# Context values from seven block products instead of eight, and the next batch's key products begun one pass early

## Chip, core and metric

The kernel runs on one core of a Trainium2 chip. The metric is device time in microseconds (us) of one execution, measured from run to run on the chip; smaller is better. A core has TensorE (PE: matmuls into PSUM, with weight loads shown apart as PEld), VectorE (DVE), ScalarE (ACT), GpSimd (POOL) and SyncE (SP), each with an instruction stream of its own that runs in order; they wait for one another through semaphores. Transfers between HBM and SBUF are issued here from SP (plain ones) and from POOL (those that add to what lies in SBUF).

## What is computed

One layer of a perceiver in f32: cross-attention from 16 x 64 query rows to 16 x 1024 context rows, self-attention, and a feed-forward part with quantized weights. The change lies in the keys and values of the cross-attention. Cut to that:

```python
def _L0_xattn_ref(query, key, value, Wq, Wk, Wv, Wo):   # key = value = ctx_4096
    b, sq, _ = query.shape                               # 16, 64, 1024
    _, sk, _ = key.shape                                 # 1024
    q = (query @ Wq).reshape(b, sq, 32, 32).transpose(0, 2, 1, 3)
    k = (key @ Wk).reshape(b, sk, 8, 32).transpose(0, 2, 1, 3)
    v = (value @ Wv).reshape(b, sk, 8, 32).transpose(0, 2, 1, 3)
    k, v = jnp.repeat(k, 4, axis=1), jnp.repeat(v, 4, axis=1)
    probs = jax.nn.softmax(jnp.einsum('bhqd,bhkd->bhqk', q, k) * 32 ** -0.5, axis=-1)
    out = jnp.einsum('bhqk,bhkd->bhqd', probs, v).transpose(0, 2, 1, 3).reshape(b, sq, 1024)
    return out @ Wo
x = x + _L0_xattn_ref(_layernorm(x), ctx_4096, ctx_4096, Wq, Wk, Wv, Wo)
```

Wk and Wv are 1024 x 256. For each of the 16 batches, `ctx @ Wk` and `ctx @ Wv` are products of 1024 x 1024 by 1024 x 256.

## The kernel before

**Passes.** The attention loop (`for n in range(2 * B)`, line 1100) runs 32 passes, two for each batch b = n // 2: an even one for the first half of the heads (g = 0) and an odd one for the second. A pass has four parts, i = 0 to 3. In a pass the kernel finishes the softmax of unit n and makes the scores of unit n + 1 (`following.by_key(i)`, matmuls of line 575). Of the scores, ScalarE copies one half (L587) while VectorE takes maxima (L591, L594), and then they change halves. After i = 3, `reduce` and `spread` send the maxima through HBM (`tops`) and bring them back to all partitions. In parts 1 and 2 of the next pass VectorE subtracts them (L618), ScalarE takes exponentials (L619), and GpSimd adds them up (`sums`: L625, L628). `values` (L637) multiplies probabilities with the context values: waves 0 and 1 in part 2, waves 2 and 3 in part 0 of the next pass, followed by `finish` (L647) and `quotients` (L656 to L666).

**Fillers.** Between these parts the kernel puts the projection of the next batch's keys and values in small steps: `fill(n)` takes n steps from a list. A step is about 1.7 us of matmuls. A pass takes 15 of them (`fill(2)` at line 1163 and `fill(1 if i == 0 and fast else 2)` at line 1178).

**Keys and values of a batch** (`project_fast`, line 388; 14 of the 16 batches). The context lies in HBM as `ctxT[b, h]`, h the half of its rows, with 8 blocks of 128 input features; `quarter(b, h, i)` is four blocks of one half, 1 MB. The keys are a 2 x 2 block product and are made by seven block products (`z5, p1, p2, z6, z7, p3, z4`, line 407) in place of eight, from sums of weight blocks (`w_sums`) and two sums of context quarters: `chained`, which grows from one quarter to four, and `paired`, of two. These sums are made by transfers that add in SBUF (`add_to_chain`, `add_to_pair`, issued from GpSimd, L381 and L384). p1 and p2 share a PSUM bank, as do z5 and p3; the rest is put together by VectorE (L445, L453, L458, L463) and GpSimd (L446). The values are made plainly (line 426): for each of 8 row tiles, 8 matmuls of 256 columns, copied by ScalarE (L434). They read the whole halves, `load_context` (L232, 2 MB each). A product is two steps, a row tile of values two.

**Order by hand.** Everything is in a manual schedule: the order in which the code emits instructions is the order on each engine. In even passes `held_back` moves `sums(1)` and `sums(2)` behind `add_to_chain(b + 1, 0, 1)` at line 1182.

**Places.** SBUF is one arena and `place(kb, shape)` a region at a fixed KB: `chained` 8, `paired` 16, `w_sums` 24, four key and value buffers from 32, the two 16 KB context halves (`stream`) at 64 and 80, the weights `wkvs` at 96. PSUM banks 0 and 1 are tags m0 and m1 and bank 2 is t1; t0 holds the outputs, w0 and w1 the scores.

**The end.** In passes 30 and 31 the fillers are `project_out` (the output projection; four steps for each of tile t and half h), 32 steps for 32 places.

Of the kernel before, what the change touches and what calls it, by code (L numbers as in the profile page):

```python
# [15 lines left out]
ALU = mybir.AluOpType  # L16
# [4 lines left out]
P = 128  # L21
DIM = 1024
B = 16
# [3 lines left out]
KC = DIM // P  # L27
HD = 32
KVD = 256
# [20 lines left out]
def kernel(  # L50
# [156 lines left out]
    chained, paired = (place(kb, [4, 512]) for kb in (8, 16))  # L207
    w_sums = place(24, [4, 4, P])
# [153 lines left out]
    def weight_sums():  # L362
        b11, b21 = (wkvs[:, 4 * i : 4 * i + 4, 0:P] for i in range(2))
        b12, b22 = (wkvs[:, 4 * i : 4 * i + 4, P : 2 * P] for i in range(2))
        s, t, z7, z4 = (w_sums[:, i] for i in range(4))
        nc.vector.tensor_tensor(s, b11, b12, ALU.subtract)
        nc.vector.tensor_tensor(z7, b12, b22, ALU.subtract)
        nc.vector.tensor_tensor(t, b22, s, ALU.add)
        nc.vector.tensor_tensor(z4, b21, t, ALU.subtract)

    def quarter(b, h, i):
        return ctxT[b, h, :, 4 * i : 4 * i + 4, :]

    def begin_chain(b):
        nc.sync.dma_start(chained, quarter(b, 1, 0))

    def begin_pair(b):
        nc.sync.dma_start(paired, quarter(b, 1, 0))

    def add_to_chain(b, h, i):  # L380
        nc.gpsimd.dma_start(chained, quarter(b, h, i), accum_op=ALU.add)  # L381

    def add_to_pair(b):
        nc.gpsimd.dma_start(paired, quarter(b, 0, 0), accum_op=ALU.add)  # L384

    later = []

    def project_fast(b):

        kT = kv_ring.next([2, NK])  # L390
        v = kv_ring.next([8, KVD])
        x_bank, z_bank, y_bank = (i % 3 for i in range(b % 3, b % 3 + 3))
        held = {}
        k11, k12, k21, k22 = (
            kT[:, g, bass.ts(h, 512)] for h, g in ((0, 0), (0, 1), (1, 0), (1, 1))
        )
        b11, b21 = (wkvs[:, 4 * i : 4 * i + 4, 0:P] for i in range(2))
        b22 = wkvs[:, 4:8, P : 2 * P]
        s, t, w7, w4 = (w_sums[:, i] for i in range(4))
        whole = lambda h, i: ctx_halves[b, h][:, 4 * i : 4 * i + 4, :]  # L400

        def product(name, n, weights, what, done, first=True):
            def piece(i):
                if i == 0 and first:
                    held[n] = bank(n, f"{name}_{b}")
                for k in (2 * i, 2 * i + 1):
                    nc.tensor.matmul(  # L407
                        held[n],
                        lhsT=weights[:, k, :],
                        rhs=what()[:, k, :],  # L410
                        start=(first and k == 0),
                        stop=(k == 3),
                        skip_group_check=not first,
                    )
                if i == 1:
                    done(held[n])

            return [lambda: piece(0), lambda: piece(1)]

        def values(h, kts, n):  # L420
            def piece(i):
                if i == 0:
                    held[n] = bank(n, f"v_{b}_{h}_{kts[0]}")
                at, half = divmod(i, 2)
                for k in range(4 * half, 4 * half + 4):
                    nc.tensor.matmul(  # L426
                        held[n][:, bass.ts(at, KVD)],
                        lhsT=ctx_halves[b, h][:, k, bass.ts(kts[at], P)],
                        rhs=wkvs[:, k, KVD:],
                        start=(k == 0),  # L430
                        stop=(k == KC - 1),
                    )
                if i == 2 * len(kts) - 1:
                    nc.scalar.copy(  # L434
                        v[:, h * 4 + kts[0] : h * 4 + kts[-1] + 1, :],
                        held[n].rearrange("p (k c) -> p k c", c=KVD)[:, : len(kts)],
                    )

            return [lambda i=i: piece(i) for i in range(2 * len(kts))]

        def copy(out):
            return lambda ps: nc.scalar.copy(out, ps)  # L442

        def after_z7(ps):
            nc.vector.tensor_tensor(k21, ps, k12, ALU.subtract)  # L445
            nc.gpsimd.tensor_tensor(k22, k21, k22, ALU.subtract)  # L446

        z5 = product("z5", z_bank, s, lambda: chained, copy(k22))
        p1 = product("p1", x_bank, b11, lambda: whole(0, 0), copy(k12))
        p2 = product("p2", x_bank, b21, lambda: whole(0, 1), copy(k11), first=False)  # L450
        z6 = product(
            "z6", y_bank, t, lambda: chained,
            lambda ps: later.append(lambda: nc.vector.tensor_tensor(k12, k12, ps, ALU.subtract)),  # L453
        )
        z7 = product("z7", y_bank, w7, lambda: paired, after_z7)
        p3 = product(
            "p3", z_bank, b22, lambda: chained,
            lambda ps: nc.vector.tensor_tensor(k12, ps, k12, ALU.add),  # L458
            first=False,
        )  # L460
        z4 = product(
            "z4", x_bank, w4, lambda: whole(1, 1),
            lambda ps: nc.vector.tensor_tensor(k21, ps, k21, ALU.add),  # L463
        )
        steps = z5 + p1 + values(0, (0,), y_bank) + p2 + z6 + values(0, (1, 2), x_bank)
        steps += z7 + p3 + z4 + values(0, (3,), y_bank)
        steps += values(1, (0, 1), z_bank) + values(1, (2, 3), x_bank)
        return kT, v, steps

# [592 lines left out]
    with tc.manual_schedule():  # L1062
# [37 lines left out]
        for n in range(2 * B):  # L1100

            b = n // 2
            if n % 2 == 0:
                fill(len(fillers))
                if b == 0:
                    load_context(1, 1)
                    kT, v, key_steps, value_steps = project(1)
                    for h in range(2):

                        for step in key_steps[h] + value_steps[h]:  # L1110
                            fillers += [step, lambda: None]
                elif b + 1 < B:
                    kT, v, steps = project_fast(b + 1)
                    fillers += steps
                if b + 1 < B:
                    tiles.append((kT, v))
                else:
                    for t in range(4):
                        load_x(xs[t], t)
                    for h in range(2):  # L1120
                        for t in (4, 5):
                            fillers += project_out(t, h)
                    for t in (0, 1):
                        for h in range(2):
                            fillers += project_out(t, h)
            following = Unit(n + 1, *tiles[(n + 1) // 2]) if n + 1 < 2 * B else None

            for i in range(4):
# [8 lines left out]
                if i == 2 and n == 2 * B - 3:  # L1137
                    wos.append(load(wo[0]))
# [4 lines left out]
                if not odd and fast:  # L1143
                    if i == 2:
                        load_context(b + 1, 1)
                if odd and b + 2 < B:
                    if i == 1:
                        begin_chain(b + 2)
                    if i == 2:
                        load_context(b + 2, 0)  # L1150
                        begin_pair(b + 2)
                if n == 1 and i == 1:
                    weight_sums()
# [6 lines left out]
                if n == 2 * B - 3 and i == 2:  # L1160
                    for t in (4, 5, 0, 1, 2, 3):
                        nc.sync.dma_start(outputs[t].rearrange("p g r c -> p (g r c)"), results[t])
                fill(2)
                if i == 0 and not odd and fast:
                    add_to_chain(b + 1, 0, 0)
# [3 lines left out]
                if i in (1, 2) and following:  # L1169
                    unit.exponentials(2 * i - 2)  # L1170
                    if i == 1 or not held_back:
                        unit.sums(2 * i - 2)
                if i == 1 and not odd and fast:
                    add_to_pair(b + 1)
# [3 lines left out]
                fill(1 if i == 0 and fast else 2)  # L1178
                if n < 8 and i == 0:
                    treat_piece()  # L1180
                if i == 2 and held_back:
                    add_to_chain(b + 1, 0, 1)
                    unit.sums(1)
                    unit.sums(2)
                if i == 1 and odd and b + 2 < B:
                    add_to_chain(b + 2, 1, 1)
# [6 lines left out]
                if i in (1, 2) and following:  # L1193
                    unit.exponentials(2 * i - 1)
                    if i == 2 or not held_back:
                        unit.sums(2 * i - 1)
                while later:
                    later.pop(0)()
# [226 lines left out]
```

## Time and profile before

Three runs took 1863.46, 1866.37 and 1866.81 us, the median 1866.37. The profiled execution has a span of 1863.3 us, from its first to its last instruction.

| what | us or share |
|---|---|
| median of the runs | 1866.37 |
| span of the profiled execution | 1863.3 |
| first scores made in pass 0 | at 186.1 |
| one batch (two passes), 9 of them in a row from 524 on | 70.2 |
| passes 2 to 9, where these two passes took longer | 72.7 to 79.8 |
| start of pass 30, the first of the last batch | 1226.8 |
| context transfers of 1 MB from POOL | 56, 11.4 from issue to landing |

How to read it: "busy" is the share of the span in which an engine had an instruction running. Matmuls are pipelined, and the end of each is modelled, so a matmul's mean is longer than the spacing between two of them. Each f32 matmul leaves two records in the trace and two weight loads. A timeline line gives start, length, engine, line, operation and count, and merges neighbours of one line. A line such as "L426 PE MATMUL v<-arena 128*128 128x256 f32 x1792 | 405.2, 382" is a group: rows times columns of the array, output form, count, busy us and mean ns of one, and after the next bar the engine's idle time ahead of the group and what ended it.

### The profile page before, as it was taken

To read this page: it belongs to the slowest core of one execution; us is meant where nothing else is said; L and a number is where in the kernel's file an instruction comes from. 1 tells how busy PE (TensorE), PEld (TensorE's weight loads), DVE (VectorE), ACT (ScalarE), POOL (GpSimd) and SP (SyncE) were. 2 spreads that over 40 slices of the span, in tenths; PEclk is the share of its full clock that TensorE was granted. 3 is DMA by queue.
4 is the path that set the end of the run, shared out by engine and by line. 5 is a ranking of instruction groups with operands and counts; after the bars stand their busy time and mean duration, and the time that the engine had idled before them with its cause. 6 is when DMAs were issued, how large, how long until landed. Compare 5 with 4: busy or idle time off the path is not lost.

```text
span 1863.3 us, 26374 instructions
## 1 busy us (share of the span) xinstructions
PE 1822.5 (98%) x10880; PEld 1080.9 (58%) x10880; DVE 1219.1 (65%) x1436; ACT 926.5 (50%) x988; POOL 885.8 (48%) x505
## 2 busy tenths in 40 slices
PE   8999999999899999999999999999999999899999
PEld 5445565565565665665665665664446454566654
DVE  3011587777877887887887887877524257775554
ACT  1233656665566776776776776544101123664221
POOL 1000446655565576576566566565503424455520
PEclk9999999999999999999999999999999999899999
DMA  9234578777687787886787787663120032243201
GB/s 346 69 106 139 187 223 271 224 231 237 188 262 196 253 254 191 263 254 195 254 252 201 251 254 202 198 186 153 36 75 19 1 77 62 51 130 109 75 29 51
DMA packets 64264, 314.65 MB, mean 169 GB/s; under 512 B 10192, under 2 KB 19344, under 8 KB 47376
## 3 DMA queue, kind: packets, MB, share of 16 engines
q1 hardware_dynamic: 52848, 242.99, 37.1%
q0 software_dynamic: 10144, 67.88, 17.2%
q10 hardware_dynamic: 1152, 2.10, 0.3%
q8 instruction: 85, 1.39, 0.3%
q14 instruction: 35, 0.29, 0.0%
HBM read 293.74 MB, written 19.20 MB: 168 GB/s over the span
## 4 chain that ended last, share of the span: by engine, by line
PE 66%; DVE 2%; POOL 2%; ACT 1%; DMA 1%; issue 1%; ACTq 0%; POOLq 0%; DVEq 0%
PE v L426 15%; PE z L407 10%; PE wo L250 6%; PE t L575 5%; PE q L250 5%; PE o L637 5%; PE d L1040 4%; PE p L407 4%; PE g L961 3%; PE gu L961 3%; PE v L740 1%; PE k L250 1%; POOL arena L628 1%; DMA arena<-in_ctxT 1%; PE o L647 1%
## 5 line engine op out<-in xcount | busy, mean ns | idle before, releaser
L628 POOL TENSOR_TENSOR arena<-arena 128x1024 f32<-128x1024 f32 x192 | 541.7, 2821 | 20.5 <-ACT arena L619 8.5
L426 PE MATMUL v<-arena 128*128 128x256 f32 x1792 | 405.2, 382 | 1.2 <-ACT arena L442 1.2
L594 DVE TENSOR_TENSOR arena<-t,arena 128x512 f32<-128x512 f32 x384 | 258.9, 688 | 211.6 <-PE t L575 155.3
L426 PEld LDWEIGHTS v<-arena 128*128 128x128 f32 x1792 | 336.8, 190 | 78.6 <-issue 29.5
L618 DVE TENSOR_TENSOR arena<-arena 128x2048 f32<-128x2048 f32 x128 | 373.5, 2958 | 4.3 <-DMA arena<-tops 4.3
L587 ACT COPY arena<-t 128x1024 f32<-128x1024 f32 x256 | 254.8, 1009 | 209.1 <-PE t L575 118.0
L619 ACT ACTIVATE arena<-arena 128x2048 f32<-128x2048 f32 x128 | 244.6, 1911 | 168.6 <-DVE arena L618 167.8
L625 POOL TENSOR_TENSOR arena<-arena 128x1024 f32<-128x1024 f32 x32 | 75.8, 2368 | 524.6 <-ACT arena L619 491.1
L407 PE MATMUL z<-arena 128*128 128x512 f32 x560 | 260.6, 608 | 11.3 <-ACT arena L442 5.3
L250 PE MATMUL q<-arena 128*128 128x512 f32 x512 | 224.6, 595 | 0.6 <-ACT arena L287 0.6
L407 PEld LDWEIGHTS z<-arena 128*128 128x128 f32 x560 | 103.2, 192 | 138.1 <-issue 117.5
L250 PEld LDWEIGHTS q<-arena 128*128 128x128 f32 x512 | 95.6, 190 | 116.4 <-issue 114.3
L575 PE MATMUL t<-arena 32*128 32x256 f32 x2048 | 146.6, 400 | 1.3 <-ACT arena L346 1.2
L961 PEld LDWEIGHTS <-arena 128*128 128x128 bf16 x1024 | 98.8, 98 | 64.7 <-issue 13.7
L591 DVE TENSOR_REDUCE arena<-t 128x512 f32<-128x1024 f32 x64 | 74.7, 1204 | 90.9 <-PE t L575 90.9
L575 PEld LDWEIGHTS t<-arena 32*128 32x128 f32 x2048 | 93.1, 184 | 66.6 <-issue 61.4
L637 PE MATMUL o<-arena 128*32 128x256 f32 x2048 | 123.8, 382 | 0.0
L250 PE MATMUL wo<-arena 128*128 128x512 f32 x256 | 112.3, 595 | 0.3 <-ACT arena L287 0.3
L407 PE MATMUL p<-arena 128*128 128x512 f32 x224 | 108.2, 605 | 0.0
L637 PEld LDWEIGHTS o<-arena 128*32 128x32 f32 x2048 | 60.0, 109 | 68.7 <-issue 32.0
L722 POOL TENSOR_TENSOR arena<-arena 128x512 f32<-128x512 f32 x20 | 33.5, 1673 | 133.6 <-DVE arena L720 133.6
L961 PE MATMUL gu<-arena 128*128 128x344 fp8e4 x544 | 85.3, 314 | 9.6 <-ACT arena L969 6.5
(146 smaller groups left out, 1974.6 us busy)
## 6 DMA issues: line engine op xcount, KB each, us to landing
arena<-in_ctxT SPq DMA_DIRECT2D x31, 2048.0 KB, 11.4
arena<-in_ctxT POOLq DMA_DIRECT2D x56, 1024.0 KB, 11.4
arena<-in_ctxT SPq DMA_DIRECT2D x28, 1024.0 KB, 12.1
arena<-tops SPq DMA_DIRECT2D x48, 512.0 KB, 4.9
arena<-in_wg SPq DMA_DIRECT2D x32, 688.0 KB, 4.5
arena<-in_wu SPq DMA_DIRECT2D x32, 688.0 KB, 6.2
arena<-in_wd SPq DMA_DIRECT2D x32, 688.0 KB, 9.2
arena<-ternary POOLq DMA_DIRECT2D x26, 344.0 KB, 3.8
```

The costliest lines, as they stand in the source:

```text
L250: nc.tensor.matmul(made[0], lhsT=lhsT(k), rhs=rhs(k), start=(k == 0), stop=(k == KC - 1))
L407: nc.tensor.matmul(held[n], lhsT=weights[:, k, :], rhs=what()[:, k, :], start=(first and k == 0), stop=(k == 3), skip_group_check=not first,)
L426: nc.tensor.matmul(held[n][:, bass.ts(at, KVD)], lhsT=ctx_halves[b, h][:, k, bass.ts(kts[at], P)], rhs=wkvs[:, k, KVD:], start=(k == 0), s ...
L575: nc.tensor.matmul(ws[jj // 2][:, jj % 2, a, :], lhsT=self.kT[rows, self.g, bass.ts(i * 2 + a, P)], rhs=two_tiles[self.b // 2 % 2][rows, s ...
L587: nc.scalar.copy(pt[:, 2 * mine : 2 * mine + 2], ws[mine])
L594: nc.vector.tensor_tensor(m, w[:, :, a], m, ALU.max)
L618: nc.vector.tensor_tensor(pt, pt, by.to_broadcast([P, 4, 2, 256]), ALU.subtract)
L619: nc.scalar.activation(pt, pt, AF.Exp)
L625: nc.gpsimd.tensor_tensor(acc, pt[:, :, 0], pt[:, :, 1], ALU.add)
L628: nc.gpsimd.tensor_tensor(acc, acc, pt[:, :, a], ALU.add)
L637: nc.tensor.matmul(self.po[bass.ts(jj, HD), 0:256], lhsT=self.v[:, kt, bass.ts(self.g * 4 + jj, HD)], rhs=self.pts[i][:, jj, a, :], start= ...
L961: nc.tensor.matmul(ps[:, :CW], lhsT=xqT[t][:, k, :], rhs=wbs[n][i][:, k, :], start=(k == 0), stop=(k == KC - 1),)
```

## The change

The values are made like the keys. `products(kind, then)` builds the seven products for keys (kind 0) and for values (kind 1). For values the context is the stationary operand as before, but each product covers one quarter of the input features and 128 output columns: for each of 4 row tiles, 4 matmuls with 128 columns. There is a second set of weight sums (`w_sums[1]`), and the block b11 of both kinds is negated in place once.

Four products of each kind, p1, z6, z7 and z4, are added up in one PSUM bank one after the other; ScalarE reads the bank after each. z5 is kept apart (`fifths`). p2 and p3 are added to the results by VectorE, and after z6 and z7 GpSimd adds or subtracts z5.

No whole half is loaded any more. Each batch loads four quarters from SP (`load_quarter`) and adds four from GpSimd (`add_quarter`), each issued when the product that last read the place is done (`then`). There are two `chains`, for even and odd batches.

The first two key products of batch b + 2 (z5, p1) become the last four steps of the passes of batch b. A pass has 14 steps in place of 15; the second `fill` of part 0 takes none. In even passes `sums(0)` comes after the second fill of part 1, and the other sums directly follow their exponentials. With the last fast batch, `project_out(4, 0)` takes the place of the products begun early; its inputs are loaded earlier.

```diff
-    chained, paired = (place(kb, [4, 512]) for kb in (8, 16))
-    w_sums = place(24, [4, 4, P])
+    chains = [place(kb, [4, 512]) for kb in (64, 8)]
+    paired, second_in, last_in = (place(kb, [4, 512]) for kb in (16, 72, 80))
+    w_sums = [place(kb, [4, 4, P]) for kb in (24, 88)]
+    fifths = [place(kb, [512]) for kb in (172, 174)]
...
+    def negate_first(kind):
+        b11 = weight_block(kind, 0, 0)
+        nc.scalar.mul(b11, b11, -1.0)
...
+    def load_quarter(dst, b, h, i):
+        if b < B:
+            nc.sync.dma_start(dst, quarter(b, h, i))
+    def add_quarter(dst, b, h, i):
+        if b < B:
+            nc.gpsimd.dma_start(dst, quarter(b, h, i), accum_op=ALU.add)
...
+                else:
+                    for kt in (2 * i, 2 * i + 1):
+                        for k in range(4):
+                            nc.tensor.matmul(
+                                ps[:, bass.ts(kt, P)],
+                                lhsT=what[:, k, bass.ts(kt, P)],
+                                rhs=weights[:, k, :],
+                                start=(first and kt == 0 and k == 0),
+                                stop=(k == 3),
+                                skip_group_check=True,
+                            )
...
+            sums = kind
+            free = (2, sums)[kind]
+            def copied(out, scale=1.0):
+                return lambda ps: nc.scalar.mul(out, ps, scale)
+            def added(out):
+                return lambda ps: nc.vector.tensor_tensor(out, ps, out, ALU.add)
+            def after_z6(ps):
+                nc.scalar.mul(o12, ps, -1.0)
+                nc.gpsimd.tensor_tensor(o12, o12, fifth, ALU.add)
+            def after_z7(ps):
+                nc.scalar.copy(o22, ps)
+                nc.gpsimd.tensor_tensor(o22, o22, fifth, ALU.subtract)
...
+                "z5": made("z5", free, s, chain, copied(fifth)),
+                "p1": made("p1", sums, b11, paired, copied(o11, -1.0)),
+                "p2": made("p2", 2, b21, second_in, added(o11)),
+                "z6": made("z6", sums, t, chain, after_z6, False),
+                "z7": made("z7", sums, w7, paired, after_z7, False),
+                "z4": made("z4", sums, w4, last_in, copied(o21), False),
+                "p3": made("p3", (2, 0)[kind], b22, chain, added(o12)),
...
+                "z6": lambda: load_quarter(second_in, b + 1, 0, 1),
+                "z4": lambda: load_quarter(paired, b + 1, 0, 0),
+                "p3": lambda: load_quarter(last_in, b + 1, 1, 1),
...
+                "z5": lambda: add_quarter(chain, b, 0, 0),
+                "p1": lambda: add_quarter(paired, b, 1, 0),
+                "p2": lambda: load_quarter(chain_of(b + 1), b + 1, 1, 0),
+                "z6": lambda: add_quarter(chain, b, 0, 1),
+                "z7": lambda: add_quarter(chain_of(b + 1), b + 1, 1, 1),
...
+        order = [values["z5"], keys["p2"], values["p1"], values["p2"], keys["z6"], values["z6"]]
+        order += [keys["z7"], values["z7"], keys["z4"], values["z4"], keys["p3"], values["p3"]]
+        return kT, v, keys["z5"] + keys["p1"], sum(order, [])
...
-                    kT, v, steps = project_fast(b + 1)
-                    fillers += steps
+                    kT, v, early_steps, steps = begun or project_fast(b + 1)
+                    fillers += steps if begun else early_steps + steps
+                    begun = project_fast(b + 2) if b + 2 < B else None
+                    if begun:
+                        fillers += begun[2]
+                    else:
+                        fillers += project_out(4, 0)
...
+                if n == 2 and i == 0:
+                    negate_first(0)
+                    weight_sums(1)
+                    negate_first(1)
+                    load_quarter(last_in, 2, 1, 1)
...
                 if i in (1, 2) and following:
                     unit.exponentials(2 * i - 2)
-                    if i == 1 or not held_back:
+                    if i == 2 or not held_back:
                         unit.sums(2 * i - 2)
...
-                fill(1 if i == 0 and fast else 2)
+                fill(0 if i == 0 and fast and b > 1 else 2)
+                if i == 1 and held_back:
+                    unit.sums(0)
...
-                if i == 2 and held_back:
-                    add_to_chain(b + 1, 0, 1)
-                    unit.sums(1)
-                    unit.sums(2)
...
                     unit.exponentials(2 * i - 1)
-                    if i == 2 or not held_back:
-                        unit.sums(2 * i - 1)
+                    unit.sums(2 * i - 1)
```

## The prediction

> **What bounds the kernel now.** I read the page's busy shares first, then the stretches, the chain of waits and the timelines of one batch. A batch is two of the 32 passes; T is the moment when TensorE starts the first scores (by_key, i = 0) of an even pass, 910.42 in the batch quoted.
>
> ```profile
> PE 1822.5 (98%) x10880; PEld 1080.9 (58%) x10880; DVE 1219.1 (65%) x1436; ACT 926.5 (50%) x988; POOL 885.8 (48%) x505
> ...
> 446.80:524.00 77.20, 71.28 (x438) 43.97 (x437) 57.75 (x63) 41.84 (x42) 43.72 (x23) 0.96 0.68 195
> ...
> 877.50:947.70 70.20, 70.20 (x458) 44.39 (x457) 57.69 (x59) 48.74 (x43) 44.36 (x22) 1.00 0.78 236
> ```
>
> The columns after the stretch are its length and the busy time of TensorE, its weight loads, VectorE, ScalarE and GpSimd, then granted clock, DMA share and GB/s. A steady batch lasts 70.20 us and TensorE is busy for all of it; VectorE has 12.5 us left, ScalarE and GpSimd over 20. Only early batches differ: 446.8 to 524.0 has 5.9 us without TensorE work and a clock of 0.96. So TensorE sets the time, and the chain of waits runs along it:
>
> ```profile
> 922.23 3.45 PE v L426 x16
> ...
> 930.38 3.43 PE z L407 x8
> ```
>
> Each matmul leaves two records. A 512-column record costs 3.43/8 = 0.429 us, a 256-column one 3.45/16 = 0.216. A batch holds 56 key records and 128 value records: 24.0 + 27.6 us.
>
> **Part 1, the value matmuls.** Eight products of 8 matmuls with 256 columns become seven products of 16 matmuls with 128 columns: 128 records go, 224 come. The trace has no f32 multiply with 128 columns; the nearest is a transpose of the same shape, with as many weight loads:
>
> ```profile
> 38.78 1.04 PE L285 MATMUL n1p<-ident,arena 128*128 128x128 f32 x8
> ...
> L426 PEld LDWEIGHTS v<-arena 128*128 128x128 f32 x1792 | 336.8, 190 | 78.6 <-issue 29.5 <-ACT arena L442 3.7 <-DVE arena L594 3.4
> ```
>
> Eight in 1.04 us, less the last one's modelled 0.27, leave 7 spacings of 0.110 us. The lower bound is half of 0.216, 0.108. The upper bound is a load of a value matmul shown as 190 ns, if it cannot hide: 0.190. Two loads following each other at 963.463 and 963.571 are 0.108 apart though the first is shown as long as 0.186, so the shown length is not the spacing. I take 0.110: 224 x 0.110 = 24.6 against 27.6, **3.0 us a batch less**, 14 batches, **-42 us**. At 0.190 it would be 42.6, +15.0 a batch, +210 us.
>
> [...]
>
> **Part 2, work off TensorE.** VectorE had four 0.68 us key sums a batch (L445, L453, L458, L463) and has four additions of the same shape (p2, p3 for keys and values): 0. ScalarE had three key copies (0.59) and five value copies (three of 0.58, two of 0.35), 4.2 us; it gets ten of 0.59, 5.9: +1.7. GpSimd had one L446 of 1.28 and gets four: +3.8; its four DMA issues stay four. On SP, two 2 MB and two 1 MB loads become four 1 MB loads. Against idle times of 12 to 26 us a batch these sizes are covered by TensorE; at nothing, unless an order makes them late. On SP each quarter is now issued behind the product that frees its place, ahead of later transfers of the maxima (tops), which wait for later scores anyway. The tightest is the first-half quarter for p1: issued when key z4 ends, 11.6 us into the odd pass, landed by the median 12.0 at 23.6, needed at 29.7. Uncovered, its 6.1 us of slack would have to go first; 0.
>
> **Part 3, the order on GpSimd.** Before, sums(1) to sums(3) of an even pass were put behind the accumulating transfers. Now they go ahead of the one that p3 needs. Queue of an even pass: transfer for z6, transfer for z7, sums(0), sums(1), sums(2), key z6 addition, sums(3), value z6 addition, **transfer for p3**, key z7, value z7, transfer for the next z5. Behind the late one wait the z7 additions and the next z5's transfer; those have 5 us to spare.
>
> ```profile
> L628 POOL TENSOR_TENSOR arena<-arena 128x1024 f32<-128x1024 f32 x192 | 541.7, 2821 | 20.5 <-ACT arena L619 8.5
> ...
> L618 DVE TENSOR_TENSOR arena<-arena 128x2048 f32<-128x2048 f32 x128 | 373.5, 2958 | 4.3 <-DMA arena<-tops 4.3
> ...
> 968.89 7.30 DVE L618 TENSOR_TENSOR arena<-arena 128x2048 f32<-128x2048 f32 x2
> ...
> 967.01 18.73 POOL L628 TENSOR_TENSOR arena<-arena 128x1024 f32<-128x1024 f32 x6
> ...
> DMA to landing us min/median/max: 9.1/11.9/16.7
> ```
>
> Where L618 and L628 meet, each loses about what the other takes: two L618 alone take 4.48 (959.72), beside L628 7.30. So I place them one after the other, 2.28 and 2.36 us.
>
> TensorE, new: i = 0 scores 1.1, one value product 3.5, outputs and sums 2.5: 7.05. i = 1 two products, 8.1. i = 2 the same and outputs 1.9, 10.0. i = 3 8.1. Pass 33.3, batch 66.6 plus some switching, 67.2 by the difference 70.2 - 3.0.
>
> VectorE: second scores at T+7.05, their maxima done at T+11; key p2 ends at T+11.7, its addition at 12.5; exponent subtractions 0 and 1 to 17.0; quotient 2.2; maxima 2.8; value p2 0.7: 22.7. GpSimd starts sums(0) when exponential 0 is out, T+16.8 (before: 927.44, T+17.0), and with sums(1) ends at 23.9. Subtraction 2 then runs to 26.2, its exponential to 28.1, subtraction 3 to 28.5. sums(2) to 33.2, key z6 34.5, sums(3) 39.2, value z6 40.5: the transfer is issued there. Lower bound if subtraction 2 is not held up: 39. Upper: with the copy of L666 (0.7 to 2.5) ahead of it, 42. Landing, from issue: 10.8, as the undisturbed ones at 845.32 and 985.71 took by the trace (10.75, 10.78); bounds 9.1, the least, and 11.9, the median. It is there at T+51.3 (48.1 to 53.9). Key p3 could start at 33.3 + 16.2 = T+49.5. **TensorE waits 1.8 us a batch, 0 to 4.4: +25 us** over 14 batches. What is late next is only the VectorE addition of p3, which subtraction 2 of the odd pass follows at about the time it had.
>
> Other waits of the same end of the pass: the next first scores need the last maxima (T+33.0 against 33.3), value z7 needs ScalarE's reading of z6 from the shared bank (33.2 against 34.4), key z7 likewise (28.7 against 29.8). I take 0; the bound is 1.3, the 0.7 of L666 and a held-up subtraction, and it does not add up, since a later second pass is a later need of p3.
>
> **Part 4, both ends.** Beginning: negating the first blocks (two ScalarE operations of 0.6) and four more VectorE sums (0.7 each) in pass 2; p1 waits some 1 us for the first: +1. The early batches have waits already (5.9 us at 505.85, from the all-reduce on GpSimd; 1 to 2 us elsewhere): taken as unchanged, -5 to +5. End: four steps of the output projection move from the last passes to pass 29, so the four that stood at i = 3 of pass 31 are gone:
>
> ```profile
> 1321.72 1.93 PE L637 MATMUL o<-arena 128*32 128x256 f32 x32
> 1323.58 7.13 PE L250 MATMUL wo<-arena 128*128 128x512 f32 x16
> 1330.64 1.93 PE L637 MATMUL o<-arena 128*32 128x256 f32 x32
> ...
> 1326.36 1.91 ACT L619 ACTIVATE arena<-arena 128x2048 f32<-128x2048 f32 x1 [2.42 <-DVE arena L618]
> ```
>
> The last values need the exponential that ends at 1328.3; without the 7.1 us TensorE is there at 1323.6 and waits 4.7: **+5**.
>
> **Sum.** -42 + 25 + 1 + 5 = -11 on the profiled 1863.3, 1852. That execution is 3 us under the median shown (its time is like the lowest run, 1863.46), so 1852 to 1855; I write 1852.
>
> **Rivals.** (a) *All waits stay hidden.* For: GpSimd is idle for 26 us a batch, and the DMA share falls with 8 MB instead of 10 a batch, so that landings near 9.1 with an issue at T+39 miss nothing. Against: the order above, with every link in a row. -42 + 6 = -36: 1828 to 1830. (b) *The p3 transfer costs more than the matmuls save*, the other side: it decides from a wait of 3.0 us less the ends' 0.4 a batch, that is an issue later than T+41.3 with a landing of 10.8. For: L666 ahead of it in every second batch, and L628's 2.82 mean where I use 2.36. Against: an issue at 40.5 by the rows. At a wait of 3.6 us: 14 x 0.6 + 6 = +14, 1878. (c) *Weight loads do not hide behind 128 columns*: 0.190 a record, +210, 2076. For: 190 ns in the row; against: the 0.108 spacing. (d) *The change saves nothing because values were not on the path*: against it stands 70.20 of 70.20; I give it 2%.
>
> **How the numbers follow.** Forecast, with a wait of 0.8 to 2.5 us: 45%; (a) 27%; (b) 22%; (c) 4%; (d) 2%. The forecast's own range is 1840 to 1864. The range, from (a) with 2 us of early waits gone to the middle of (b): 1826 to 1874. What a measurement can tell from no change is 0.2%, 3.7 us, so 1862.6 and 1870.1 divide: from the forecast 40 of its 45 count as faster and 5 as the same; (a) all faster; (b) 4 the same, 18 slower; (c) slower; (d) the same. Faster 0.67, same 0.11, slower 0.22.
>
> **What would show it.** Value records at 0.110 us; a steady batch of about 69 us with one TensorE gap, in the odd pass, ahead of key p3 and put down to an in_ctxT transfer issued on GpSimd near T+40. No such gap and 67.2 us: (a). A gap over 3 us: (b). Records near 0.19: (c). Gaps ahead of the first scores or of z7 put down to VectorE or ScalarE would mean that I ranked the waits wrongly, and a batch above 70.2 without (b)'s gap would break the whole account.

## The result, and the profile after

| | runs | median us | ratio to the kernel before, 95% interval |
|---|---|---|---|
| before | 4 | 1866.59 (1863.46 to 1870.04) | |
| changed | 4 | 1909.66 (1905.68 to 1912.64) | 1.0232 (1.0212 to 1.0251) |

The changed kernel is 43 us slower. Its profiled execution spans 1910.9 us, 47.6 more than the one before. First the busy shares and the granted clock in 40 slices, from its page:

```profile
PE 1809.5 (95%) x12224; PEld 1119.0 (59%) x12224; DVE 1199.2 (63%) x1440; ACT 941.5 (49%) x1018; POOL 888.6 (47%) x547
...
PEclk9999999999989999999999999999999999999999
```

TensorE is busy 13 us less than before in a span that is 48 us longer: the work went down, and idle time came in. Where, by passes (from first scores to first scores; the last column is time at half clock; all in us):

| kernel | passes 0 to 9 | 10 to 28 | 29 | from 30 on | at half clock, first 1400 us |
|---|---|---|---|---|---|
| before | 373.4 | 667.4 | 35.1 | 601.3 | 6.8 |
| changed | 392.0 | 688.0 | 41.6 | 603.3 | 61.4 |

Counted like this, pass 30 of the kernel before starts at 1261.9; the 1226.8 in the table ahead of the prediction is the start of pass 29. Of its pairs of passes from 2 to 9 the longest takes 78.8; 79.8 is the stretch of passes 7 and 8.

Two of those passes one after the other, from the timeline of TensorE:

```profile
675.75 3.84 PE L423 MATMUL p<-arena 128*128 128x128 f32 x32
...
699.45 3.70 PE L412 MATMUL p<-arena 128*128 128x512 f32 x8
...
709.36 1.15 PE L604 MATMUL t<-arena 32*128 32x256 f32 x16 [0.78 <-DVE arena L623]
710.43 3.70 PE L412 MATMUL z<-arena 128*128 128x512 f32 x8
714.78 3.70 PE L412 MATMUL p<-arena 128*128 128x512 f32 x8 [0.65 <-DVE arena L454]
721.36 1.15 PE L604 MATMUL t<-arena 32*128 32x256 f32 x16 [2.88 <-DVE arena L623]
```

Lines have moved: L423 is the value products, L412 the key products, L604 the scores, L623 their maxima, L454 the additions of p2 and p3, L647, L648 and L657 subtraction, exponential and sums. 32 value records take 3.84 us, and key p3 starts at 699.45 on time. From the second half of this odd pass (13) to the next first scores TensorE waits for VectorE three times, 4.3 us in all: twice the scores for maxima, and in between key p1 for an addition that reads its bank. Over the kernel, from the table of waits of ScalarE (waiting engine and line, releaser: us, times, longest):

```profile
ACT arena L559 <- DMA ternary<-arena: 46.9, 14, 10.4
```

The trace of before has no wait of this kind. It belongs to work that the change did not touch. `treat_piece` quantizes a piece of feed-forward weights: ScalarE scales it (L555) and takes its Sign (L559) into one place of 1.3 KB, from which SP writes it to HBM (L560). The next Sign must not overwrite the place before that write has landed. ScalarE, SP and GpSimd in pass 13:

```profile
695.40 1.52 ACT L555 ACTIVATE arena<-arena,magic,inverse 128x1376 f32<-128x1376 f32 x1
701.34 1.44 ACT L559 ACTIVATE arena<-arena,magic 128x1376 fp8e4<-128x1376 f32 x1 [4.42 <-DMA ternary<-arena]
702.69 1.89 ACT L648 ACTIVATE arena<-arena 128x2048 f32<-128x2048 f32 x1
```
```profile
687.77 0.38 SPq L1195 DMA_DIRECT2D arena<-spilled  x1
691.57 0.32 SPq L560 DMA_DIRECT2D ternary<-arena  x1
691.93 1.36 SPq L543 DMA_DIRECT2D arena<-in_wg  x1
693.41 0.85 SPq L388 DMA_DIRECT2D arena<-in_ctxT  x1
```
```profile
689.70 0.86 POOL L392 DMA_DIRECT2D arena<-in_ctxT  x1
690.30 2.77 POOL L462 TENSOR_TENSOR arena<-arena 128x512 f32<-128x512 f32 x2
692.76 1.16 POOL L392 DMA_DIRECT2D arena<-in_ctxT  x1
```

Within 6 us of the write's issue at 691.57 stand two accumulating transfers of 1 MB, a load of 1 MB, a weight piece of 0.7 MB and a spilled tile of 0.5 MB. The write of 172 KB lands 9.7 us after its issue; the corresponding one before the change (952.78, in the same place of an odd pass) took 2.3. Writes as slow as this one are not new. Over all 48, before the change:

```profile
DMA to landing us min/median/max: 1.8/7.1/12.4
```

But in the batches from pass 10 on those that took 7.7 to 10.8 us had 15 us or more until ScalarE was ready for the next Sign, and those with a Sign 6.6 us behind them landed in at most 3.4. The new order puts the slow landing where the next Sign follows closely. In pass 13 ScalarE stands still for 4.42 us with exponential 0, ready since 696.3, behind the Sign. What follows is a line of late steps, VectorE's part of which reads:

```profile
707.80 1.42 DVE L623 TENSOR_TENSOR arena<-t,arena 128x512 f32<-128x512 f32 x2 [5.88 <-ACT arena L616]
709.13 0.68 DVE L454 TENSOR_TENSOR arena<-p,arena 128x512 f32<-128x512 f32 x1
709.73 4.40 DVE L647 TENSOR_TENSOR arena<-arena 128x2048 f32<-128x2048 f32 x1
...
719.80 1.42 DVE L623 TENSOR_TENSOR arena<-t,arena 128x512 f32<-128x512 f32 x2 [1.55 <-ACT arena L616]
```

VectorE waits 5.88 us for ScalarE's copy of the scores, which is queued behind the exponentials; then every later maximum is late, and TensorE waits for the scores' banks. And a gap of TensorE has a second price. Length, TensorE busy, the other engines, and third from the end the granted clock, just before and after the first scores of 721.36:

```profile
719.40:722.80 3.40, 1.44 (x19) 1.13 (x20) 2.90 (x4) 2.48 (x5) 3.32 (x2) 1.00 0.00 0
722.80:726.20 3.40, 3.40 (x19) 3.40 (x18) 3.29 (x8) 0.81 (x2) 3.32 (x2) 0.50 0.01 1
```

The 3.40 us after the gap run at half clock, so the next pass loses 1.7 more (i = 0 of pass 14 takes 8.8 us instead of 7.1). Up to 1400 us the changed kernel has 14 such stretches, 61.4 us, worth up to 31 by an estimate (half of it); before had one, of 6.8, at its gap of 5.3 us (505.89). Work at half clock counts as busy (3.40 of 3.40 us in the second row), so the 13 us by which TensorE's busy time fell hide a larger saving, by the same estimate up to 40.

### The profile page after: what moved, and what is told of

Same layout as the page of the kernel before. It is cut to its first block, busy times and chain, and to the rows that moved or that the text cites. A ratio compares the mean times of both kernels' runs of the same rounds, so it can differ in the third digit from the quotient of the medians.

```text
span 1910.9 us, 29195 instructions
## 1 busy us (share of the span) xinstructions
PE 1809.5 (95%) x12224; PEld 1119.0 (59%) x12224; DVE 1199.2 (63%) x1440; ACT 941.5 (49%) x1018; POOL 888.6 (47%) x547
## 4 chain that ended last, share of the span: by engine, by line
PE 52%; DVE 22%; DMA 10%; ACT 9%; issue 5%; POOL 2%; SPq 0%; ACTq 0%; DVEq 0%; POOLq 0%
PE q L252 11%; DVE arena L647 9%; DVE arena L623 5%; PE wo L252 5%; PE p L412 5%; PE d L1069 4%; DMA ternary<-arena 3%; PE k L252 3%; PE g L990 3%; PE p L423 3%; ACT arena L648 3%; PE gu L990 3%; PE t L604 3%; PE z L423 3%; DMA arena<-in_ctxT 3%
## 5 line engine op out<-in xcount | busy, mean ns | idle before, releaser
L657 POOL TENSOR_TENSOR arena<-arena 128x1024 f32<-128x1024 f32 x192 | 473.6, 2467 | 116.7 <-ACT arena L648 105.4
L623 DVE TENSOR_TENSOR arena<-t,arena 128x512 f32<-128x512 f32 x384 | 261.1, 689 | 291.9 <-PE t L604 162.3
L647 DVE TENSOR_TENSOR arena<-arena 128x2048 f32<-128x2048 f32 x128 | 351.3, 2774 | 6.5 <-DMA arena<-tops 6.5
L648 ACT ACTIVATE arena<-arena 128x2048 f32<-128x2048 f32 x128 | 244.0, 1907 | 194.7 <-DVE arena L647 194.4
L412 PE MATMUL p<-arena 128*128 128x512 f32 x672 | 315.9, 614 | 23.9 <-DMA arena<-in_ctxT 16.2
L423 PEld LDWEIGHTS p<-arena 128*128 128x128 f32 x2688 | 309.9, 192 | 33.8 <-issue 29.4
L423 PE MATMUL p<-arena 128*128 128x128 f32 x2688 | 317.7, 277 | 0.0
L654 POOL TENSOR_TENSOR arena<-arena 128x1024 f32<-128x1024 f32 x32 | 76.6, 2395 | 362.0 <-ACT arena L648 222.9
L412 PEld LDWEIGHTS p<-arena 128*128 128x128 f32 x672 | 125.1, 195 | 173.6 <-issue 143.3
L604 PE MATMUL t<-arena 32*128 32x256 f32 x2048 | 149.7, 407 | 34.9 <-DVE arena L623 34.4
L604 PEld LDWEIGHTS t<-arena 32*128 32x128 f32 x2048 | 95.4, 187 | 95.8 <-issue 36.4
L392 POOL DMA_DIRECT2D arena<-in_ctxT x56 | 52.9, 945 | 145.4 <-PE p L423 119.0
## 6 DMA issues: line engine op xcount, KB each, us to landing
arena<-in_ctxT POOLq DMA_DIRECT2D x56, 1024.0 KB, 10.3
arena<-in_wg SPq DMA_DIRECT2D x32, 688.0 KB, 4.5
arena<-in_wu SPq DMA_DIRECT2D x32, 688.0 KB, 6.1
arena<-in_wd SPq DMA_DIRECT2D x32, 688.0 KB, 8.0
```

The costliest lines, as they stand in the source:

```text
L412: nc.tensor.matmul(ps, lhsT=weights[:, k, :], rhs=what[:, k, :], start=(first and k == 0), stop=(k == 3), skip_group_check=True,)
L423: nc.tensor.matmul(ps[:, bass.ts(kt, P)], lhsT=what[:, k, bass.ts(kt, P)], rhs=weights[:, k, :], start=(first and kt == 0 and k == 0), sto ...
L604: nc.tensor.matmul(ws[jj // 2][:, jj % 2, a, :], lhsT=self.kT[rows, self.g, bass.ts(i * 2 + a, P)], rhs=two_tiles[self.b // 2 % 2][rows, s ...
L623: nc.vector.tensor_tensor(m, w[:, :, a], m, ALU.max)
L647: nc.vector.tensor_tensor(pt, pt, by.to_broadcast([P, 4, 2, 256]), ALU.subtract)
L648: nc.scalar.activation(pt, pt, AF.Exp)
```

## The experiments

Three theories: (A) a transfer on which ScalarE waits lands late because transfers meet; the rest follows down the line, with the half clock at its end. (B) GpSimd's four added operations a batch hold VectorE up (in the prediction's rows two subtractions take 7.30 us beside GpSimd's sums and 4.48 alone). (C) the predicted wait for p3's transfer is the cost. Ratios are to the kernel before, run on the same chip.

**A second place for the codes.**

```diff
-    ws_ring, ternary_at = Ring(184, 195.75), 190.71875
+    ws_ring, ternary_ring = Ring(184, 195.75), Ring(190.71875, 189.375)
...
-            q = place(ternary_at, [HALF], F8)
+            q = ternary_ring.next([HALF], F8)
```

> The changed kernel with one edit: the quantized codes of a weight piece (L559's output, 1.3 KB) get a second place, used in turn, so that ScalarE's Sign of the next piece does not wait until the last piece's codes are written to HBM. Theory A (transfers that GpSimd issues late meet others at the start of odd passes, the codes' write lands 10 us late, ScalarE stands still 4.4 to 6.2 us in five odd passes and 10.4 us in pass 9, the exponentials and the score maxima are late, and TensorE's gaps of about 3 us are each followed by 3.4 us at half clock): the holds are gone, those passes fall from 38.4 to 40.1 us to about 35, 20 to 30 us less in all, 1880 to 1890. [...] Theory C (the predicted wait for p3's transfer is the cost): 5 us less at most.

Measured: 1867.88 (1861.54 to 1874.35), 1.0012 (0.9997 to 1.0027). 1.3 KB of memory give back 42 us, more than A expected. TensorE's waits for maxima, with one place and with two:

```profile
PE t L604 <- DVE arena L623: 34.4, 21, 2.9
```
```profile
PE t L604 <- DVE arena L623: 11.4, 14, 2.9
```

That is 23 us, and time at half clock up to 1400 us falls from 61.4 to 34.1, worth up to 14 more (half of the difference, an estimate). Two batches in a row, in the columns used above:

```profile
608.80:676.70 67.90, 67.62 (x553) 45.88 (x552) 56.05 (x59) 49.62 (x44) 46.81 (x25) 1.00 0.67 193
676.70:744.50 67.80, 67.55 (x553) 45.88 (x552) 55.99 (x59) 49.63 (x44) 42.09 (x23) 1.00 0.77 233
```

A batch takes 67.9 us, TensorE busy for all but 0.3, where before took 70.20 and the changed kernel 69.8 to 75.7. The write is not faster (it still takes up to 16.0 us to land); nobody waits for it. Passes 10 to 28 take 650.7 us, 16.7 less than before. What keeps the total at that of before are passes 0 to 9 (387.2, 13.8 more) and 29 (41.2, 6.1 more).

**p3's transfer ahead of sums(3).** The sums of wave 3 move behind value z6's step in even passes, with one place for the codes and with two.

```diff
+                if i == 3 and held_back:
+                    unit.sums(3)
                 fill(0 if i == 0 and fast and b > 1 else 2)
...
                     unit.exponentials(2 * i - 1)
-                    unit.sums(2 * i - 1)
+                    if i == 1 or not held_back:
+                        unit.sums(2 * i - 1)
```

> The changed kernel with one edit: in even passes sums(3) is emitted behind the step of value z6, so that GpSimd issues p3's accumulating transfer some 4 us earlier (two 2.36 us additions no longer lie ahead of it). Theory A: the two transfers of an odd pass's beginning no longer meet, the codes' write lands at 8 us or less, the holds shrink to half or less: 10 to 20 us less, and waits of TensorE for in_ctxT in passes 3, 5 and 7 (3 us each) go too; but finish may wait 1 us for the later sums. Theory B: nothing, within 4 us. Theory C: only the waits ahead of key p3 go, about 3 us in each of passes 3, 5 and 7 and 1 us elsewhere, with their half clock some 15 us.

> Both edits, the second place for the codes and sums(3) behind value z6. Theory A: 30 to 40 us less than the changed kernel, 1868 to 1880, with steady batches near 68.5 to 70 us and half the stretches at half clock gone. Theory B: within 8 us of the changed kernel. Theory C: as p3's earlier transfer alone.

Measured: 1915.34 (1.0258, 1.0235 to 1.0282) with one place, 1884.62 (1.0102, 1.0087 to 1.0118) with two. A miss for A's numbers and for C. The wait for L560 falls only from 46.9 to 31.2 us: in pass 17 the write still lands 10.8 us after its issue, with one accumulating transfer beside it instead of two, a spilled tile (issued 1.2 us ahead), a weight piece and a quarter. And TensorE waits for the later sums at `finish`, about 1 us in odd passes, so they take 35.2 us with two places and 34.0 without this edit. It is no cure; only pass 29 gains (34.8): there p3's transfer is now issued ahead of the 2 MB of projection weights, and it lands in 7.9 us, where behind them it took 15.2 and 15.8.

**Without GpSimd's additions.**

```diff
-                nc.gpsimd.tensor_tensor(o12, o12, fifth, ALU.add)
...
-                nc.gpsimd.tensor_tensor(o22, o22, fifth, ALU.subtract)
```

> The changed kernel without the four GpSimd additions a batch that add z5 to the results of z6 and z7, for keys and for values (so half of each batch's keys and values lack z5). Theory B: VectorE and GpSimd are free of them, 25 us less or more. Theory A: GpSimd's queue is 5 us a batch shorter and the transfers are issued 1.3 to 2.6 us earlier: 2 to 10 us less, the holds of ScalarE remain above 2 us. Theory C: about the same as A.

Measured: 1933.41 (1.0366, 1.0349 to 1.0383), 24 us slower than with the additions. With the run of the second place, which keeps the additions and gives the time back, B falls. A did not foresee the sign, but its mechanism shows: without the two operations of L462 between them, GpSimd issues the two transfers 0.6 us apart (699.33 and 699.92 in pass 13) instead of 3.1, and the wait grows:

```profile
ACT arena L557 <- DMA ternary<-arena: 59.3, 11, 8.1
```

**Without p3's transfer**, one place for the codes.

```diff
-                "z6": lambda: add_quarter(chain, b, 0, 1),
```

> The changed kernel, one place for the codes, without the accumulating transfer that p3 needs (so p3 of keys and values multiplies a sum of three quarters instead of four). Theory A (the write lands late because two transfers of 1 MB issued by GpSimd at the start of odd passes run at the same time as it): the write at i = 0 of odd passes lands at 6.5 us or less instead of 9.7 to 10.8, ScalarE is held under 2 us, 25 us less or more. If the write is late because of what lies ahead of it on SP's queue, or of the weight load behind it: its landing stays at 9 us or more and the time within 10 us.

Measured: 1846.11 (0.9886, 0.9867 to 0.9906), 64 us under the changed kernel. The write's landing and the wait for it:

```profile
DMA to landing us min/median/max: 1.8/5.8/8.4
```
```profile
ACT arena L558 <- DMA ternary<-arena: 4.6, 5, 1.8
```

With one of the two transfers away the hold is nearly gone, and SP's queue is as it was: its order is not what makes the write late. In the place of the 9.7 us, in odd passes 11 to 27, the write now lands in at most 4.0. The transfer that is left is issued 0.5 to 0.6 us behind it there, while p3's stood 1.9 us ahead; so p3's transfer ahead of the write makes it late, and whether it takes the second one as well is not shown. This kernel also lies 22 us under the one with two places. That TensorE never waits for p3's transfer either fits: its waits for context transfers were 13.3 us there, with 34.1 us at half clock against 10.2 here. This is a second cost of the same transfer, near what C had said, though the traffic that is missing may have a part in it.

**The kernel before with a second place.** The same edit there.

> The kernel before with the second place for the codes and nothing else. In its trace ScalarE's Sign is nowhere held more than 0.3 us. Theory A: nothing, 1863 to 1869. If the place for the codes limited that kernel too: 10 us less or more.

Measured: 1865.97 (1.0000, 0.9990 to 1.0011). The single place cost nothing as long as no Sign followed closely behind a slow write.

**The two ends.** On top of the second place: the projection weights at other times; then the weight pieces of passes 0 to 7 spread; then the first weights in pass 28; then the transfer ahead of the result's own work.

```diff
-                if i == 0 and n == 2 * B - 3:
+                if i == 1 and n == 2 * B - 3:
                     wos.append(load(wo[0]))
+                if i == 3 and n == 2 * B - 3:
+                    wos.append(load(wo[1]))
...
-            if n == 2 * B - 3:
-                wos.append(load(wo[1]))
```

> The second place for the codes, and the two output-projection weights loaded at other times: the first at i = 1 of pass 29 instead of i = 0, the second at i = 3 of pass 29 instead of its end. With the second place alone TensorE waits 6.3 us in pass 29 for p3's transfer (landed 15 us after its issue, beside the 2 MB weights) and 4.3 us in pass 30 for the second weights, with 10 us at half clock after them. Theory A (transfers that meet, then waits, then half clock): pass 29 falls from 41.2 to about 36, the wait in pass 30 goes, 10 to 14 us less than with the second place alone, 1854 to 1858. If the transfers were not what is waited for: no change, 1868.

Measured: 1862.65 (0.9983, 0.9972 to 0.9994), 5 us less instead of 10 to 14. The wait for the second weights is gone. Pass 29 still takes 41.5, but its half of the theory was not tested: in the trace the first weights are issued 5.8 us into the pass with this change and without it. Ahead of them on SP's queue, which issued them in the order of the code, stand the maxima of pass 28 and nothing of pass 29, so one part later in the code was no later on the chip.

```diff
-                if n < 8 and i == 0:
+                if n < 8 and i == 3:
                     treat_piece()
```

> As the run before it, and in passes 0 to 7 the second of the two weight pieces of i = 0 is treated at i = 3, so that ScalarE does not wait for its load (19.7 us of such waits for in_wd between 222 and 500). Theory A (ScalarE held by a transfer is what makes the maxima late in early passes too): passes 2 to 7 fall from 42.0, 41.8, 38.2, 38.1, 37.2, 37.5 by 1 to 3 us each, 6 to 15 us less, 1840 to 1850. If these passes are slow because of p3's transfer alone: 0 to 4 us less.

Measured: 1858.07 (0.9949, 0.9931 to 0.9967), 5 us less. Passes 4 and 6 fall to 33.8, the length without a wait; 5 and 7 stay at 38.7 and 38.0, with waits of 3.2 and 2.5 us ahead of key p3 in TensorE's rows (the expectations count 0.3 to 0.4 us more for such a wait). So both reasons hold there, one in even passes, the other in odd ones.

```diff
-                if i == 1 and n == 2 * B - 3:
+                if i == 3 and n == 2 * B - 4:
                     wos.append(load(wo[0]))
```

> Second place for the codes, pieces spread in passes 0 to 7, second projection weights at i = 3 of pass 29, and the first ones moved from i = 1 of pass 29 to i = 3 of pass 28, where no quarters of a next batch are loaded. Theory A: the first move, from i = 0 to i = 1, left p3's transfer of pass 29 beside the 2 MB (landed 15 us after its issue, 5.8 us of waiting, 6.8 us at half clock); now it lands in about 10, pass 29 falls from 42.0 to 34 to 36, 6 to 8 us less than 1858. If something other than the weights makes that landing late: 0 to 2 us less.

Measured: 1854.40 (0.9930, 0.9918 to 0.9943), the best version: 11 us under before by the medians (1865.34 here). Pass 29 takes 39.9, not 34 to 36: 3.6 us of wait remain, with 13.3 us from issue to landing. The trace shows the first weights and p3's transfer still side by side:

```profile
1216.62 0.32 SPq L642 DMA_DIRECT2D arena<-tops  x1
1217.05 0.37 SPq L234 DMA_DIRECT2D arena<-in_wo  x1
```
```profile
1218.96 0.85 POOL L392 DMA_DIRECT2D arena<-in_ctxT  x1
```

Written into part 3 of pass 28, the weights stand on SP behind the maxima of that pass (L642) and are issued 4.8 us into pass 29, one us earlier than without this change. That they make p3's transfer late fits the runs in which it was issued ahead of them; it was not tried further.

```diff
-                    done(ps)
                     if then:
                         then()
+                    done(ps)
```

> As the run before it, and each product's transfer is emitted ahead of what is done with its result, so that on GpSimd p3's transfer no longer stands behind value z6's addition (1.3 us) and, before that, behind ScalarE's reading of value z6. Theory A: TensorE's waits ahead of key p3 in passes 5, 7, 9 and 29 (1.5 to 3.5 us) get 1.3 us shorter or more, two or three stretches at half clock go: 4 to 10 us less than the run before it. If landing times alone make these waits: 0 to 2 us less.

Measured: 1860.06 (0.9962, 0.9948 to 0.9975), 6 us more, not less. The waits ahead of key p3 in passes 5 and 7 fall by only 0.7 and 0.4 us (to 2.5 and 2.3), and pass 29 has 4.4: issued 1.2 us earlier in it, p3's transfer takes 15.4 us instead of 13.3 and lands later. The 6 us lie mostly in pass 3 (2.1 more) and from pass 30 on (3.5 more); why stays open.

## Why the prediction was wrong

**Right: the matmuls.** 0.110 us a value record was predicted; a row of 32 in 3.84 us, less the last one's modelled 0.28 and 0.1 for the first load, makes 0.112. A pass without a wait takes 33.8 (predicted 33.3), a batch 67.6 (67.2). The saving is 2.6 us a batch instead of 3.0, and no load failed to hide: shown as 0.192 us, the loads of this row start 0.112 apart like its records.

**Right: the order on GpSimd and the time of issue.** In pass 12 (T = 649.11) p3's transfer is issued at T+40.6; predicted T+40.5. It lands in 9.6 us, and key p3 is not late. In steady batches the wait is 0.6 us, in passes 17 and 21 alone, against 1.8 in each (with the second place 1.9 and 1.1); the 25 us were put in the wrong place, since the long ones come where p3's transfer took 11.6 to 15.2 us to land (8.0 to 10.3 in the odd passes 11 to 27): 2.8 and 2.5 us in passes 5 and 7, 1.4 in 9, 5.4 in 29. Rival (b) named the right transfer, for without it the kernel takes 1846; but TensorE's wait for it, its mechanism, is the smaller part, and its 1878 was too low.

**Wrong: "at nothing, unless an order makes them late" for ScalarE, and "I take 0" for the next first scores.** That is the step that failed: the order did make ScalarE late, 46.9 us in 14 holds, and taking the holds away gave back 42 us. I asked of each transfer whether its own reader would be late, with landing times taken from undisturbed transfers. I did not ask what else was on the DMA engines at the time to which the order moved it, nor who waits for that. ScalarE's 20 us of idle time were no cover: in its order the Sign held 4.42 us held exponential 0 (ready since 696.3, started at 702.69), the copy of the scores and so VectorE, 5.88 us. Two of the signs of a wrong ranking named in the prediction came: gaps ahead of first scores put down to VectorE, and batches above 70.2 with key p3 on time. The even pass went as worked out (last maxima at T+33.0 by the rows, 682.15 - 649.11 = 33.04 in the trace); the odd pass, which I had not followed beyond the addition of p3, has the wait, up to 2.9 us at the first scores and 4.3 in the pass shown. The bound of 1.3 that I gave left it out.

**Left out: the clock.** The window that I showed of before had it, 0.96 beside 5.9 us without work. I read it as a stall of that place and gave gaps of 2 to 3 us no second price. In the changed kernel gaps of 2.1 to 2.9 us can have 3.4 us at half clock behind them (below).

**The ends.** Start: p1 waits 1.2 us for the negation (predicted 1). End: the last values wait 2.2 us for their exponential (predicted 4.7), but the waits in pass 29 and for the second projection weights, both taken at about nothing, are 5.4 and 3.7 us, with 6.8 and 3.4 us at half clock.

**The alternatives.** With the second place the steady passes behave as rival (a) said: 67.9 a batch. The changed kernel as it stands is outside the range on the high side. With the second place 1868 lies inside it, but by luck: the 25 us of waits are nearly absent from the steady batches, and passes 0 to 9 and 29, taken as nearly unchanged, are 20 us longer.

## What to carry to other kernels

When an edit moves transfers, list everything that is in flight at the new time, small writes included, and for each the engine that waits for it in order; a buffer that was used once more before its write had landed turned a transfer of 172 KB into a stall of the whole line here (46.9 us in 14 holds of ScalarE). Read in the trace when a moved transfer is issued: written into two different parts of pass 29, the first projection weights were issued at the same time, 5.8 us into the pass. Where one engine is busy all the time, a wait of 3 us on it can cost more than itself (behind three gaps of 2.88 us stood 3.4 us at a clock of 0.50), so look at the granted clock behind each gap. An idle share covers added work only if nothing in that engine's own order waits: ScalarE's 20 us a batch did not cover a hold of 4.42.

## What the runs showed of the hardware

How long a gap of TensorE is does not alone decide whether the clock falls. After gaps of 2.9 us (721.36, 865.10, 1011.39) it was 0.50 for 3.4 us, and after one of 2.1 (1230.51) too; around the gap of 5.4 us in pass 29 for 6.8. After 2.0 us (649.11) it stayed at 1.00, and so it did after another of 2.9:

```profile
1160.75 1.15 PE L604 MATMUL t<-arena 32*128 32x256 f32 x16 [2.88 <-DVE arena L623]
```
```profile
1160.70:1194.60 33.90, 33.85 (x288) 23.93 (x288) 27.87 (x30) 23.04 (x21) 18.29 (x10) 1.00 0.70 193
```

In the trace's clock records the stretches at half clock begin on one grid: 722.82, 866.18, 1012.95 and 1231.40 lie 42, 43 and 64 steps of 3.413 us apart. The grid steps just ahead of those four have 1.46, 1.08, 1.56 and 1.32 us of TensorE work, so by an estimate they hold 1.85 to 2.3 us without it. The gap at 649.11 has 1.4 us of its 2.0 in its larger step, and the one at 1160.75 is cut into 1.86 and 1.02: at about 1.85 us a step the trace does not separate the two. The stretches of 3.4 and 6.8 us are one and two steps long. So 1.85 us without work in a step of 3.4 stood ahead of half clock once, and 1.86 stood ahead of the full clock; what decides between them is not shown.

An f32 multiply with 128 columns keeps 0.112 us a record, with a weight load of 128x128 shown as 0.192 us beside each:

```profile
L423 PEld LDWEIGHTS p<-arena 128*128 128x128 f32 x2688 | 309.9, 192 | 33.8 <-issue 29.4
```
